# A list scheduler's costs, tolerances and due times in a four-layer transformer kernel

## The chip, the cores and the metric

One core of a Trainium2 chip. The metric is device time in microseconds, the median of repeated executions; lower is better.

## The reference

All is float32. `x` is 8 batches of 512 rows of 512. Four steps, each added to `x` through a layernorm:

```
x = x + LN(attn0(LN(x)))   # scores = xn^T xn (512x512), softmax over rows, xn @ weights^T
x = x + LN(ffn0(LN(x)))    # x @ sum of 8 factors / sqrt(8) + bias
x = x + LN(attn1(LN(x)))   # 8 query heads, 2 key/value heads of 64, softmax, Wo, residual inside
x = x + LN(ffn1(LN(x)))    # silu(x Wg^T * gs) * (x Wu^T * us), then Wd^T * ds; 1408 hidden units, weights -1, 0 or 1
```

`LN` is a layernorm without weights. The weights of the last step hold only -1, 0 and 1.

## The kernel before, in words

**Tiling.** A batch is four tiles of 128 rows by 512. Each of the four steps is a stage function that doesn't issue instructions but records operations: `stage_attn0` (L603 transposes, L642 scores, L671 context), `stage_ffn0` (L603, L693), `stage_attn1` (L855 queries, L825 keys, L836 values, L884 scores of two heads, L915 transposes of their softmax, L946 weighted values, L972 output projection) and `stage_ffn1` (L1094 gate and up products of one slice of 128 hidden units, L1162 down product).

**Tilings and types on TensorE.** Most matmuls use the array as 128x128. The scores of the second attention and their transposes (L884, L915) use it as two halves of 64 rows, `64x128`; the weighted values (L946) as two halves of 64 columns, `128x64`. The last step (L1094, L1162) runs in float32r: each activation is split in two float32r parts (L1035 on ScalarE, L1044 on VectorE), [...] because the weights' low bits are zero. The kernel looks at those bits (`look_at_low_bits`), and a second program in plain float32 stands behind a branch for weights where they aren't; with these inputs it isn't run.

**Vector work.** A layernorm is statistics (L510, L515, or L730, L738), `ve` and a power on GpSimd (L519, L526), normalizing (L534), and the addition to `x` on GpSimd (L553). A softmax is a maximum (L567), the exponential on ScalarE (L574), a reciprocal (L584) and a scaling (L591). ScalarE copies what TensorE transposes from PSUM to SBUF (L607, L927), and computes the sigmoid (L1114); changing between the sigmoid and the exponential loads a table. VectorE gates (L1124, L1133).

**Loads.** SP's queue loads `x`, factors and attention weights and stores the output. GpSimd's queue loads the slices of the gate and up weights (`wgu`, four buffers of 256 KB, L381) and `wd`. PSUM is five banks `f` and three `g`.

**Order.** `Recorder.add` notes an operation with its engine, its estimated duration, what it depends on, and `state`: for ScalarE the table it needs, for TensorE the tiling. Its priority is a due time from `due()`: the batch's number plus a constant of its kind (`DUE`), a shift for some batches (`SHIFT`) and a slope over the steps inside. One unit is one batch. `Recorder.issue` then plans: it keeps a clock for each engine, finds for each ready operation when it could start, takes of each engine's operations those that could start within `SLACK` of the first, and of these the one that is due first. A change of state delays the start by `CHANGE` (1.3 on ScalarE, 0.1 on TensorE), and on TensorE it also counts `STAY` (0.0066) in the priority. The order that comes out is the order in which each engine executes; buffers are assigned in it too. In the last batch (`EARLY`) the second attention and the last step are split into halves of the rows, so the first `FEW` = 4 slices run with 256 columns.

Of the kernel before, what the change touches and what calls it, by code (L numbers as in the profile page):

```python
# [53 lines left out]
class Recorder:  # L54
# [1 line left out]
    LAT = {"PE": 0.22, "ACT": 0.08, "DVE": 0.08, "POOL": 0.08, "SP": 2.6}  # L56
    OWN = 0.05

    CHANGE = {"ACT": 1.3, "PE": 0.1}

    def __init__(self):
        self.ops = []
# [2 lines left out]
    def add(self, eng, dur, fn, reads=(), writes=(), room=(), after=(), state=None, lat=None):  # L65

        op = Op()
        op.eng, op.dur, op.fn, op.state = eng, dur, fn, state  # L70
        op.lat = self.LAT[eng] if lat is None else lat
        op.prio = self.prio
        op.succ, op.wait, op.ready = [], 0, 0.0
        op.n = len(self.ops)
        before = set(after)
        bufs = set(room)
        for ref in reads:
            b, k = ref if isinstance(ref, tuple) else (ref, None)
            bufs.add(b)
            for part, w in b.writers.items():  # L80
                if k is None or part is None or part == k:
                    before.add(w)
            b.readers.setdefault(k, []).append(op)
        for ref in writes:
            b, k = ref if isinstance(ref, tuple) else (ref, None)
            bufs.add(b)
            for part, w in b.writers.items():
                if k is None or part is None or part == k:
                    before.add(w)
            for part, rs in b.readers.items():  # L90
                if k is None or part is None or part == k:
                    before.update(rs)
            if k is None:
                b.writers, b.readers = {None: op}, {}
            else:
                b.writers[k] = op
                b.readers[k] = []
        before.discard(op)
        op.bufs = sorted(bufs, key=lambda b: b.n)
        for b in op.bufs:  # L100
            b.left += 1
        op.wait = len(before)
        for o in sorted(before, key=lambda o: o.n):
            o.succ.append(op)
        self.ops.append(op)
        return op

    def issue(self, places, slack):

        free = {tag: [(0.0, i, t) for i, t in enumerate(ts_)] for tag, ts_ in places.items()}  # L110
        clock = dict.fromkeys(self.LAT, 0.0)
        state = {}
        ready = {e: [] for e in self.LAT}
        for op in self.ops:
            if not op.wait:
                ready[op.eng].append(op)
        left = len(self.ops)
        order = []

        def start(op):  # L120
            at = max(op.ready, clock[op.eng])
            need = {}
            for b in op.bufs:
                if b.t is None:
                    need[b.tag] = need.get(b.tag, 0) + 1
            for tag, n in need.items():
                f = free[tag]
                if len(f) < n:
                    return None
                at = max(at, f[n - 1][0])  # L130
            if op.state is not None and op.state != state.get(op.eng):
                at += self.CHANGE[op.eng]
            return at

        while left:
            best = None
            for e, ops in ready.items():
                able = [(s, op.prio, op.n, op) for op in ops if (s := start(op)) is not None]
                if not able:
                    continue  # L140
                first = min(able)[0]
                held = state.get(e)
                pick = min(
                    (p + (STAY.get(e, 0.0) if op.state not in (None, held) else 0.0), n, s, op)
                    for s, p, n, op in able
                    if s <= first + slack
                )
                if best is None or (pick[2], pick[1]) < best[:2]:
                    best = (pick[2], pick[1], pick[3])
            if best is None:  # L150
                stuck = sorted(
                    (op.prio, e, [b.tag for b in op.bufs if b.t is None])
                    for e, ops in ready.items()
                    for op in ops
                )
                raise RuntimeError(f"no operation can start, for want of buffers: {stuck[:12]}")
            at, _, op = best
            e = op.eng
            ready[e].remove(op)
            for b in op.bufs:  # L160
                if b.t is None:
                    _, _, b.t = free[b.tag].pop(0)
            if op.state is not None:
                state[e] = op.state
            clock[e] = at + op.dur
            end = at + op.dur + op.lat
            op.fn()
            left -= 1
            for b in op.bufs:
                b.left -= 1  # L170
                b.end = max(b.end, end)
                if not b.left:
                    free[b.tag].append((b.end, len(order), b.t))
                    free[b.tag].sort(key=lambda x: x[:2])
            order.append(at)
            for o in op.succ:
                o.wait -= 1
                o.ready = max(o.ready, at + op.dur + self.OWN if o.eng == e else end)
                if not o.wait:
                    ready[o.eng].append(o)  # L180
        return clock
# [61 lines left out]
def layers(  # L243
# [22 lines left out]
    split = flag is not None  # L266
# [97 lines left out]
    fsum = Fixed("fsum", BIG)  # L364
# [7 lines left out]
    wd = Fixed("wd", [P, NI, D], FAST)  # L372
# [185 lines left out]
    def mm(bank, us, go, reads, room=(), state="128x128"):  # L558
        return add("PE", us, go, reads=reads, writes=[bank], room=room, state=state)
# [489 lines left out]
            )  # L1049

    def stage_ffn1(x, b, after):
        PASS = 0.23 if split else 0.86
        xs = [Buf("hl") for _ in range(1 + split)]
        hds = [Buf(f"hd{c}") for c in range(len(CUTS))]

# [6 lines left out]
        known, products = set(), []  # L1062
        for q, (toks, its) in enumerate(rounds):
# [14 lines left out]
            for c, (lo, hi) in enumerate(CUTS):  # L1078
                for it in range(lo, hi):
# [9 lines left out]
                    def product(bank, w, cut=cut):  # L1089
                        def go():  # L1090
                            n = 0
                            for kt in range(KT):
                                for d in xs:
                                    nc.tensor.matmul(  # L1094
                                        bank.t[:, cut],
                                        w.t[:, kt, :],
                                        d.t[:, kt, cut],
                                        start=(n == 0),
                                        stop=(n == KT * len(xs) - 1),
                                    )  # L1100
                                    n += 1

                        return go


                    us = PASS * KT * len(xs) * len(toks) / NT
                    mm(pg, us, product(pg, wg), [wg, *mine], room=[hds[c]])
                    products.append(mm(pu, us, product(pu, wu), [wu, *mine]))
                    gsc = lambda it=it: gs.t[:, it : it + 1]
                    usc = lambda it=it: us_.t[:, it : it + 1]  # L1110
                    add(
# [27 lines left out]
        for t in range(NT):  # L1139
            po = Buf("g")  # L1140
            for c, (lo, hi) in enumerate(CUTS):
# [17 lines left out]
                def down(ops=ops, po=po, lo=lo, hi=hi):  # L1159
# [14 lines left out]
                    reads=[*{buf_of(o): 0 for o in ops}, wd],  # L1174
                    writes=[po],
                    after=products,
                    state="128x128",
                )
            z = Buf("z")
            add(  # L1180
# [36 lines left out]


DUE = {
    "x": (0.0595,),  # L1220
    "fsum": (0.0844, 0.01),
    "scales": (0.2884,),
    "wd": (1.1173,),
    "low": (1.3155, 0.01),
    "a0.norm": (0.0803,),
    "a0.row": (0.0175, 0.0195),
    "a0.out": (0.2134, 0.0139),
    "f0": (0.3719, 0.0331),
    "a1.norm": (0.6166, 0.0452),
    "a1.kv": (0.691,),  # L1230
    "a1.q": (0.6808, 0.1115),
    "a1.row": (0.6967, 0.0723, 0.036, 0.0208),
    "a1.mix": (0.7469, 0.0737, 0.036),
    "a1.out": (1.0283, 0.0236),
    "e1.row": (0.6591, 0.039, 0.1695, 0.0034),
    "e1.mix": (0.9942, 0.0607, 0.1848),
    "e1.out": (0.9884, 0.018, 0.141),
    "f1.norm": (1.7342, 0.0089),
    "f1.gate": (1.716, 0.0146),
    "f1.down": (1.935, 0.019, 0.0131),  # L1240
    "h1.norm": (1.7316, -0.021, 0.095),
    "h1.gate": (1.1851, -0.0129, 0.0932),
    "h1.down": (1.935, 0.0236, 0.0091),
}

SHIFT = {
    ("a0", 0): -0.112,
    ("a1", 0): 0.183,
    ("f0", 0): 0.0174,
    ("f1", 0): -0.0585,  # L1250
    ("a0", 1): -0.1017,
    ("a1", 1): -0.011,
    ("f1", 1): -0.0293,
    ("x", 1): 0.0585,
    ("f1", 2): -0.0302,
    ("f0", -2): 0.0561,
    ("f1", -2): -0.0165,
    ("f0", -1): 0.1176,
}

STAY = {"PE": 0.0066}
SLACK = 0.1198
FSUM_POOL = (0, 3)
EARLY = (-1,)
FEW = 4
# [54 lines left out]
```

## Time and profile before

| | |
|---|---|
| median of 3 runs | 1549.88 us (1546.22 to 1550.55) |
| profiled execution | 1548.17 us |
| its span, first to last instruction | 1546.4 us |
| granted TensorE clock, mean | 0.993 |
| first matmul starts | 7.8 us |
| TensorE busy | 1499.7 us, 8050 matmul records |
| VectorE, ScalarE, GpSimd busy | 1078.3, 688.6, 576.2 us |
| table loads on ScalarE | 60 of 1283 ns |
| DMA moved | 107.98 MB |

The page gives busy time by engine, the same in 40 slices of the span, the chain of work that ended last, and groups of instructions by source line. A float32 matmul leaves two records, a float32r matmul and a transpose one each. The end of a matmul record is modelled, so the distance from one start to the next tells more than a record's length. Line numbers are those of the kernel before; in the kernel after, all the lines named here stand 6 higher (L603 is L609 there).

### The profile page before, as it was taken

The numbers are of one execution on the slowest core, as the hardware profiler recorded it, in microseconds if no ns is written. First come the engines' busy times: TensorE is split into PE (matmuls) and PEld (weight loads), VectorE is DVE, ScalarE is ACT, GpSimd is POOL, SyncE is SP. The second block draws the span as 40 slices with busy tenths as digits, with TensorE's granted clock in tenths as the row PEclk, the third lists the DMA queues.
The fourth block names the chain that finished last, engine by engine and source line by source line (L and its number), as shares of the span: only waits on it lengthen the run. The fifth ranks groups of instructions, "written<-read, shape, count | busy, mean of one in ns | idle before, by whom it ended". The sixth has DMA issues, their size and how long they took to land.

```text
span 1546.4 us, 22104 instructions
## 1 busy us (share of the span) xinstructions
PE 1499.7 (97%) x8050; PEld 927.7 (60%) x8050; DVE 1078.3 (70%) x2227; ACT 688.6 (45%) x1440; POOL 576.2 (37%) x884
## 2 busy tenths in 40 slices
PE   6899999999999999999999999999999999999986
PEld 3454567655666656665566656666566665666675
DVE  5889966778567785587846787467865678558735
ACT  2145537642376324663256523574226642276211
POOL 6803352137411473025720366102651026411431
PEclk9999999999999999999999999999999999999998
DMA  9560054012421125213141122411233002430370
GB/s 332 151 184 8 1 123 82 28 42 62 89 55 36 49 54 104 40 42 75 30 93 35 49 68 55 87 30 49 55 76 75 29 21 58 86 69 21 78 141 30
DMA packets 156695, 107.98 MB, mean 70 GB/s; under 512 B 7073, under 2 KB 137121, under 8 KB 156577
## 3 DMA queue, kind: packets, MB, share of 16 engines
q0 software_dynamic: 98736, 51.13, 17.5%
q1 hardware_dynamic: 57840, 55.34, 11.7%
q8 instruction: 66, 1.08, 0.3%
q14 instruction: 53, 0.43, 0.1%
HBM read 98.06 MB, written 8.39 MB: 69 GB/s over the span
## 4 chain that ended last, share of the span: by engine, by line
PE 74%; POOL 11%; DVE 10%; issue 2%; DMA 2%; ACT 0%; SPq 0%; POOLq 0%; DVEq 0%
PE g L1094 16%; PE g L1162 11%; PE f L884 8%; PE f L946 8%; PE f L855 7%; PE f L972 5%; PE f L915 5%; POOL rstd L526 3%; PE f L642 3%; POOL x L553 3%; PE f L671 3%; DVE row L534 2%; PE f L603 2%; DVE st L510 2%; PE f L836 2%
## 5 line engine op out<-in xcount | busy, mean ns | idle before, releaser
L1094 PE MATMUL g<-hl,wgu 128*128 128x512 f32 (+1 forms) x1408 | 343.2, 395 | 5.5 <-DMA wgu<-in_gate_t 3.3
L1094 PEld LDWEIGHTS g<-hl,wgu 128*128 128x128 f32 x1408 | 254.7, 189 | 80.8 <-issue 12.5
L567 DVE TENSOR_REDUCE s<-f 128x1 f32<-128x512 f32 x288 | 184.8, 684 | 165.3 <-PE f L884 143.4
L519 POOL TENSOR_SCALAR ve<-mv 128x1 f32<-128x1 f32 x224 | 69.5, 311 | 563.7 <-DVE mv L515 534.2
L574 ACT ACTIVATE e<-f,s 128x512 f32<-128x512 f32 x288 | 195.9, 688 | 74.6 <-DVE s L567 73.8
L1162 PE MATMUL g<-wd,hl 128*128 128x512 f32 x704 | 180.6, 407 | 2.2 <-ACT hl L1035 1.7
L553 POOL TENSOR_TENSOR x<-x,z 128x512 f32<-128x512 f32 x120 | 158.1, 1318 | 59.5 <-DVE z L534 38.1
L927 ACT COPY big<-f 128x512 f32<-128x512 f32 x256 | 134.8, 594 | 61.5 <-PE f L915 59.5
L591 DVE TENSOR_SCALAR e<-e,s 128x512 f32<-128x512 f32 x288 | 152.3, 529 | 10.2
L1162 PEld LDWEIGHTS g<-wd,hl 128*128 128x128 f32 x704 | 129.3, 190 | 48.0 <-issue 16.0
L526 POOL TENSOR_TENSOR rstd<-ve,mhalf 128x1 f32<-128x1 f32 x224 | 143.5, 641 | 18.1
L381 POOL DMA_DIRECT2D wgu<-in_gate_t x92 | 73.4, 798 | 167.1 <-PE g L1094 161.8
L884 PE MATMUL f<-kv,big 64*128 64x512 f32 x512 | 132.9, 619 | 0.0
L1124 DVE SCALAR_TENSOR_TENSOR sig<-g,gs,sig 128x512 f32<-128x512 f32 x84 | 62.8, 748 | 95.1 <-ACT sig L1114 95.1
L946 PE MATMUL f<-big,kv 128*64 128x256 f32 x1024 | 124.0, 385 | 0.0
L381 POOL DMA_DIRECT2D wgu<-in_up_t x92 | 70.6, 768 | 129.6 <-PE g L1094 127.7
L693 PE MATMUL f<-fsum,rT 128*128 128x512 f32 x256 | 116.7, 603 | 1.3 <-ACT rT L607 1.2
L855 PE MATMUL f<-big,ws 128*128 128x512 f32 x256 | 118.0, 605 | 0.0
L972 PE MATMUL f<-ws,big 128*128 128x512 f32 x256 | 115.8, 596 | 0.0
L671 PE MATMUL f<-big,big 128*128 128x512 f32 x256 | 114.0, 602 | 0.7 <-ACT big L607 0.7
L946 PEld LDWEIGHTS f<-big,kv 128*64 128x64 f32 x1024 | 68.1, 136 | 68.3 <-issue 19.6
L915 PEld LDWEIGHTS f<-ident,e 64*128 64x128 f32 x2048 | 71.9, 139 | 48.5 <-issue 38.3
(89 smaller groups left out, 1973.8 us busy)
## 6 DMA issues: line engine op xcount, KB each, us to landing
wgu<-in_gate_t POOLq DMA_DIRECT2D x92, 256.0 KB, 3.4
wgu<-in_up_t POOLq DMA_DIRECT2D x92, 256.0 KB, 3.5
x<-in_x SPq DMA_DIRECT2D x32, 256.0 KB, 2.7
ws<-in_wq_t SPq DMA_DIRECT2D x32, 256.0 KB, 2.8
ws<-in_wo_t SPq DMA_DIRECT2D x32, 256.0 KB, 2.6
out<-x SPq DMA_DIRECT2D x32, 256.0 KB, 2.0
hd<-in_factors SPq DMA_DIRECT2D x28, 256.0 KB, 7.2
wd<-in_down_t POOLq DMA_DIRECT2D x11, 256.0 KB, 7.7
```

The lines of the kernel that those rows point to most:

```text
L526: lambda: nc.gpsimd.tensor_tensor(rstd.t[:, :], ve.t[:, :], mhalf, ALU.pow),
L553: lambda: on.tensor_tensor(ap(xt), ap(xt), y.t[:, :], ALU.add),
L567: lambda: nc.vector.tensor_reduce(nmax.t[:, :], sc.t[:, :], AX.X, ALU.max, negate=True),
L574: lambda: nc.scalar.activation(e.t[:, :], sc.t[:, :], AF.Exp, bias=nmax.t[:, :], accum_out=tot.t[:, :]),
L591: lambda: nc.vector.tensor_scalar(e.t[:, :], e.t[:, :], rtot.t[:, :], None, ALU.mult),
L671: nc.tensor.matmul(po.t[:, :], xnT.t[:, j, ts(t, P)], wT.t[:, j, :], start=(j == 0), stop=(j == KT - 1),)
L855: nc.tensor.matmul(pq.t[:, :], wq.t[:, kt, :], hT.t[:, kt, :], start=(kt == 0), stop=(kt == KT - 1),)
L884: nc.tensor.matmul(scs[g].t[:, :], qT.t[gp, i, ts(s, P)], kT.t[gp, :], start=True, stop=True,)
L946: nc.tensor.matmul(po.t[gp, : 2 * P], v.t[:, t * P + g * DH : t * P + (g + 1) * DH], columns_of(aT)[:, g * NT + t, :], start=(t == 0), sto ...
L972: nc.tensor.matmul(po.t[:, :], qT.t[:, i, ts(t, P)], flat(wos[i].t), start=(i == 0), stop=(i == NPAIR - 1),)
L1094: nc.tensor.matmul(bank.t[:, cut], w.t[:, kt, :], d.t[:, kt, cut], start=(n == 0), stop=(n == KT * len(xs) - 1),)
L1162: nc.tensor.matmul(po.t[:, :], ap(o)[:, it - lo, :], wd.t[:, it, :], start=(it == 0 and k == 0), stop=(it == NI - 1 and k == len(ops) - 1),)
```

## The change

Four parts of the scheduler and all its constants.

- `CHANGE` becomes a function of the state before and the new one. On TensorE it counts 0.09 for a change of tiling and 0.12 for an entry to float32r, so up to 0.21; leaving float32r for float32 of the same tiling counts nothing. The products of the last step get the state `128x128r` in the program that runs. Their estimated duration for one pass goes from 0.23 to 0.229.
- In the choice, `STAY` (now 0.2148 on TensorE) is multiplied by this cost, where before 0.0066 was added for any change.
- The tolerance `SLACK` is a number for each engine.
- Operations under 0.3 us have `SMALL` taken off their due time; `SMALL` is 0 in the changed kernel.
- All of `DUE` and `SHIFT` are new numbers.

```diff
-    CHANGE = {"ACT": 1.3, "PE": 0.1}
+    @staticmethod
+    def change(eng, old, new):
+        if new is None or new == old:
+            return 0.0
+        if eng == "ACT":
+            return 1.3
+        return 0.09 * (old is None or old.strip("r") != new.strip("r")) + 0.12 * new.endswith("r")
...
-        op.prio = self.prio
+        op.prio = self.prio - (SMALL if dur < 0.3 else 0.0)
...
-            if op.state is not None and op.state != state.get(op.eng):
-                at += self.CHANGE[op.eng]
-            return at
+            return at + self.change(op.eng, state.get(op.eng), op.state)
...
-                held = state.get(e)
+                stay = STAY.get(e, 0.0)
                 pick = min(
-                    (p + (STAY.get(e, 0.0) if op.state not in (None, held) else 0.0), n, s, op)
+                    (p + stay * self.change(e, state.get(e), op.state), n, s, op)
                     for s, p, n, op in able
-                    if s <= first + slack
+                    if s <= first + slack[e]
                 )
...
-        PASS = 0.23 if split else 0.86
+        PASS, array = (0.229, "128x128r") if split else (0.86, "128x128")
...
-                    mm(pg, us, product(pg, wg), [wg, *mine], room=[hds[c]])
-                    products.append(mm(pu, us, product(pu, wu), [wu, *mine]))
+                    mm(pg, us, product(pg, wg), [wg, *mine], room=[hds[c]], state=array)
+                    products.append(mm(pu, us, product(pu, wu), [wu, *mine], state=array))
...
 DUE = {
-    "x": (0.0595,),
-    "fsum": (0.0844, 0.01),
+    "x": (-0.2533,),
+    "fsum": (0.3114, 0.0312),
...
-    "e1.row": (0.6591, 0.039, 0.1695, 0.0034),
+    "e1.row": (0.0386, 0.0334, 0.5419, -0.0515),
...
-    "h1.gate": (1.1851, -0.0129, 0.0932),
+    "h1.gate": (1.4039, 0.0198, 0.4807),
...
-STAY = {"PE": 0.0066}
-SLACK = 0.1198
+STAY = {"PE": 0.2148}
+SLACK = {"PE": 0.1422, "ACT": 0.1218, "DVE": 0.1385, "POOL": 0.1719, "SP": 0.1357}
+SMALL = 0
```

The down product's `state="128x128"` also becomes `state=array`. `SHIFT` goes from 12 entries to 19.

More of the change, by code (lines that the diff above doesn't have):

```diff
@@ L1176, in stage_ffn1 @@
                     after=products,
-                    state="128x128",
+                    state=array,
                 )
@@ L1219 @@
 DUE = {
-    "x": (0.0595,),
-    "fsum": (0.0844, 0.01),
[L1222 to L1234, printed above, removed]
-    "e1.row": (0.6591, 0.039, 0.1695, 0.0034),
@@ L1236 @@
[L1236 to L1241, printed above, removed]
-    "h1.gate": (1.1851, -0.0129, 0.0932),
-    "h1.down": (1.935, 0.0236, 0.0091),
+    "x": (-0.2533,),
+    "fsum": (0.3114, 0.0312),
+    "scales": (0.6222,),
+    "wd": (1.213,),
+    "low": (1.2859, 0.014),
+    "a0.norm": (0.0439,),
+    "a0.row": (0.0055, 0.0111),
@@ new lines @@
+    "a0.out": (0.1758, 0.0279),
+    "f0": (0.2466, 0.1151),
+    "a1.norm": (0.6218, 0.0433),
+    "a1.kv": (0.7585,),
+    "a1.q": (0.695, 0.101),
+    "a1.row": (0.7101, 0.0703, 0.0322, 0.0233),
+    "a1.mix": (0.6497, 0.0532, 0.0436),
+    "a1.out": (1.0313, 0.0174),
+    "e1.row": (0.0386, 0.0334, 0.5419, -0.0515),
+    "e1.mix": (1.0181, 0.019, 0.1484),
+    "e1.out": (0.6386, 0.0105, 0.1575),
+    "f1.norm": (1.9819, 0.0044),
+    "f1.gate": (1.7154, 0.0078),
+    "f1.down": (1.9213, 0.0376, 0.0083),
@@ L1244 @@
+    "h1.norm": (1.0667, -0.2027, 0.1913),
+    "h1.gate": (1.4039, 0.0198, 0.4807),
+    "h1.down": (1.9405, 0.0086, 0.0044),
 }
 SHIFT = {
[L1247 to L1258, printed above, removed]
-}
-STAY = {"PE": 0.0066}
-SLACK = 0.1198
+    ("a0", 0): 0.072,
@@ new lines @@
+    ("a1", 0): 0.2005,
+    ("f0", 0): 0.0598,
+    ("f1", 0): -0.0823,
+    ("x", 0): 0.0884,
+    ("a0", 1): -0.0745,
+    ("f0", 1): -0.1916,
+    ("f1", 1): 0.0114,
+    ("x", 1): 0.1766,
+    ("a0", 2): 0.0102,
+    ("f0", 2): -0.1129,
+    ("x", 2): -0.2536,
+    ("a1", -2): 0.0132,
+    ("f1", -2): -0.0341,
+    ("x", -2): 0.0641,
+    ("a1", -1): -0.0323,
+    ("f0", -1): 0.112,
+    ("f1", -1): -0.1277,
+    ("x", -1): 0.134,
+}
+STAY = {"PE": 0.2148}
+SLACK = {"PE": 0.1422, "ACT": 0.1218, "DVE": 0.1385, "POOL": 0.1719, "SP": 0.1357}
```

## The prediction

> **What bounds the kernel now.** I read the page's first two parts, the waits of TensorE, TensorE's timeline in one batch, then the chain. The lines of the page:
>
> ```profile
> PE 1499.7 (97%) x8050; PEld 927.7 (60%) x8050; DVE 1078.3 (70%) x2227; ACT 688.6 (45%) x1440; POOL 576.2 (37%) x884
> ...
> PE   6899999999999999999999999999999999999986
> DVE  5889966778567785587846787467865678558735
> ```
>
> TensorE (PE) is at nine tenths in all slices but the first two and last two. Next comes what it still waits for:
>
> ```profile
> PE f L603 <- DVE row L534: 12.8, 12, 3.4
> PE f L603 <- DVE big L534: 7.8, 1, 7.8
> PE f L603 <- DVE e L591: 3.6, 3, 1.7
> PE g L1094 <- DMA wgu<-in_gate_t: 3.3, 4, 1.3
> ```
>
> 7.8 us are the start; the rest is mostly the first batch (gaps of 3.4, 1.7 and 2.2 us up to 208 us) and the tail (1.0, 1.3, 0.7, 0.6, 1.3 us from 1465 us). In the steady batches I find one gap of 0.67 us each (L1094 to L603). The windows say the same: 198.8 of 200 us busy. So no wait is worth much in the steady part; only a shorter TensorE program is. "Busy" hides pauses between matmuls, so I took starts. TensorE's timeline, columns start, length, line, tiling, shape, records:
>
> ```profile
> 406.88 0.60 PE L603 MATMUL f<-ident,row 128*128 128x128 f32 x4
> 407.24 2.10 PE L1094 MATMUL g<-hl,wgu 128*128 128x512 f32 x8
> 409.17 3.60 PE L855 MATMUL f<-big,ws 128*128 128x512 f32 x8
> 412.61 3.60 PE L825 MATMUL f<-big,ws 128*128 128x512 f32 x8
> ...
> 427.28 1.21 PE L915 MATMUL f<-ident,e 64*128 64x64 f32 x32
> 428.42 2.12 PE L1094 MATMUL g<-hl,wgu 128*128 128x512 f32 x8
> 430.47 1.99 PE L884 MATMUL f<-kv,big 64*128 64x512 f32 x8
> ```
>
> ```profile
> 475.50 0.71 PE L915 MATMUL f<-ident,e 64*128 64x64 f32 x16
> 476.14 3.70 PE L855 MATMUL f<-big,ws 128*128 128x512 f32 x8
> 479.77 0.71 PE L915 MATMUL f<-ident,e 64*128 64x64 f32 x16
> 480.32 1.96 PE L884 MATMUL f<-kv,big 64*128 64x512 f32 x8
> ```
>
> The same group L855 takes 412.61 - 409.17 = 3.44 us start to start between groups of its own tiling (128*128), and 479.77 - 476.14 = 3.63 us between two of 64*128. It is entered and left by a change, and each change splits over its two groups: 0.09 us where one is left (L915: 0.64 us before L855, 0.55 us before L884 of its own tiling), the rest, about 0.10, at the first matmul after it. So **one change of tiling costs about 0.20 us** when it enters a 128*128 group. The float32r product L1094 agrees: 430.47 - 428.42 = 2.05 us for 8 passes between changes. Entered from a float32 group of the same tiling it takes 1.93 us, but the L603 ahead of it is shorter (0.36 us where four of 0.109 us make 0.44), so 1.85 net, against 8 x 0.229 = 1.83: **the entry to float32r by itself costs about 0.02 us**, not the 0.12 that the new model counts.
>
> [...]
>
> **The change part by part.** No arithmetic, tile or buffer changes; only the order on each engine. So I built the changed program and counted in its order.
>
> 1. *Changes of tiling* in the program that runs (the fallback behind the check of low bits doesn't): 345 before, 303 after. Into 128*128 (both data types) 137 to 117, into 64*128 147 to 125, into 128*64 61 to 61. A steady batch has 45 before and 39 after. The 20 into 128*128 at 0.20 us make -4.0. The 22 into 64*128 lie between 0.10 (only the leaving is seen for L915) and 0.20: -2.2 to -4.4, and I take the middle, -3.3. TensorE is the bound, so all of it is on the path: **-7.3 us**, ends -6.2 and -8.4.
> 2. *Entries to float32r*: 140 to 103, but those from float32 of the same tiling, the only ones not counted above, 43 to 40: 3 x 0.02, nothing. If the 0.12 of the model were right, -0.4.
> 3. *Short operations first*: SMALL is 0, so no priority moves. This part does nothing: 0.
> 4. *Table loads of ScalarE*: 60 to 50, -12.8 us of ScalarE, which is 45% busy. Off the path: 0. Its cover is TensorE's continuous work; were it gone, 1.3 us each.
> 5. *Tolerances and due times* move everything else, so waits come and go. Steady batch: the transposes of the second of the last three attention rows stood 11.6 us of matmuls after the product they depend on and waited 0.67 us; they get 13.9 us, so that wait goes (seen in 4 batches, -2.7). The transposes of the fourth row ahead of the factor product (L693) had 11.6 us after the end of their L671 group and get 7.7. Their chain, read in the timeline at 1107.5 to 1116.4 (statistics, POOL's power, normalizing, POOL's add, the same again), takes 8.9 us, but the new order puts two vector operations that stood ahead of it behind it: estimate +0.4 us in 6 or 7 batches, +2.6, ends 0 and +8. Together about 0.
> 6. *Queues*. SP's first 19 loads keep their order; the second batch's x moves ahead of three small constants, all well before use. POOL's weight loads (0.8 us to issue, 3.4 to land) follow the products. The new order has longer unbroken runs of L1094: 152 passes in the first batch where the longest before was 48, 40 to 72 later, 192 in the tail where 176 stood. One buffer's cycle is 1.83 us of use, 0.3 to the issue, 3.44 to landing, 0.14 to the start: 5.7 us, and four buffers give 4 x 1.83 = 7.3. So 1.6 us of slack for a late issue: 0, at worst +1 per turn of four in the long run of 19 slices, +5.
> 7. *Tail*. 16 half-width passes (1.9 us) move from between the last two projections to behind the last row's transposes, where TensorE waited for the copies: -1.9. But ten half-width slices now follow each other, 4 x 0.96 = 3.8 us for a cycle of 4.8: about +1 twice. Net 0, ends -2 and +3.
>
> Sum: -7.3 + 0 + 0 + 0. I add +0.3 for a few waits I can't place: -7. The profiled run took 1548.17 us (span 1546.4 and 1.8 around it), 1.7 below the median of the runs shown: **1541 us**.
>
> **The rivals.**
> *The gain is eaten by waits.* Parts 5 to 7 at their upper ends are +8, +5, +3; half of these is +8, so about 1548. For it: the new order sometimes has less cover, and rows waiting for L534 are already the largest wait. Against: where I measured cover, it shrank in one place and grew in another.
> *ScalarE is late at one place, and the kernel slower.* In 20 places (three in each steady batch) the new order has attention transposes L915, two score matmuls L884, and at once the next L915 into a bank that the first L915 filled. In the trace the first of the two copies L927 ends 0.84 us after the last transposes start, the second 1.33; the L884 pair covers about 1.0. The bank reused is that of the first copy, so nothing waits if ScalarE is idle then. If an exponential (0.69 + 0.20 us) stands ahead, each place waits 0.84 + 0.89 - 1.0 = 0.73 us, 20 x 0.73 = 14.6: 1548.2 - 7.3 + 14.6 = 1555.5. It decides from 0.37 us a place. Against: in the order of ScalarE the exponential or copy ahead of it has 2 us of matmuls to finish in.
> *More is gained than the changes.* The start and the first batch hold some 15 us of gaps; a better overlap there (the first L1094 comes after 17 us more of other matmuls, so the rows ahead of it are less urgent) gives -6 more: 1535.
> *The change does not do what it says*: of its named parts one is idle (part 3) and one misprices (0.12 for 0.02); the count of changes nevertheless falls, so this doesn't end at no change by itself.
>
> **How the numbers follow.** Against the median of 1549.88, 0.3% is 4.6 us, about what a measurement here can tell from no change. Forecast, 1537 to 1545: 0.56. More gained, under 1537: 0.12. Eaten, 1545 to 1554: 0.20. Slower, over 1554.5: 0.12. So faster 0.68, same 0.20, slower 0.12. The range leaves out the best twentieth or so and the slower case: 1533 to 1551.
>
> **What would show it.** Right: a steady batch, from its first L825 to the next one's (969.99 to 1156.73 us in the chain, so 186.7), at about 185.5 us with the same number of passes, 50 table loads, L855 still 3.44 and 3.63 us. L603's waits for L534 stay near 13 us. Wrong: new lines among TensorE's waits, such as L915 for ACT's L927, L1094 for the DMA above 5 us, or L603 for L534 above 18 us. If the time falls by much more than 8 us, the price of a change or the gaps of the first batch were undercounted.

## The result, and the profile after

| | before | after |
|---|---|---|
| median | 1549.88 us | 1530.61 us (1527.48 to 1531.42, 5 runs) |
| ratio after to before | | 0.9881, 95% interval 0.9865 to 0.9896 |
| profiled execution, its span | 1548.17, 1546.4 us | 1531.37, 1529.6 us |

The kernel is 1.2% faster, 19.3 us by the medians and 16.8 us by the two profiled executions. The forecast was 8.9 us less by the medians and 7 by the profile. The direction is right, the size is less than half of it, and 1530.6 lies below the range. The sums below are made on the two profiled executions.

The page after, the lines that answer to those shown of before (all lines of code stand 6 higher):

```profile
PE 1485.2 (97%) x8050; PEld 926.3 (61%) x8050; DVE 1078.3 (70%) x2227; ACT 677.2 (44%) x1430; POOL 577.8 (38%) x884
...
PE   6899999999999999999999999999999999999987
...
DVE  5889964788547785588845978459874678657745
```

The same 8050 records keep TensorE busy 14.5 us less, at the same 97%. So most of the gain doesn't show as idle time on this view: it is inside "busy". The waits of TensorE after:

```profile
PE f L609 <- DVE big L540: 10.6, 2, 9.3
PE f L609 <- DVE row L540: 6.1, 10, 1.5
PE f L609 <- DVE e L597: 5.6, 10, 1.7
PE g L1100 <- DMA wgu<-in_gate_t: 2.3, 2, 1.5
```

Rows waiting for the layernorm fell from 12.8 us to 6.1, the longest from 3.4 to 1.5; the start (9.3 of the first line) came 1.4 later. That is no effect of the change: tail_out and tail_fill below, whose order in the head is the after's matmul for matmul, start at 9.1 and 8.4 us, and fill_before, with the order of before, at 9.1 where before has 7.8. TensorE's timeline in a steady batch, with start, length, line, tiling, shape and records:

```profile
421.98 1.21 PE L921 MATMUL f<-ident,e 64*128 64x64 f32 x32
423.12 3.70 PE L861 MATMUL f<-big,ws 128*128 128x512 f32 x8
426.75 1.95 PE L952 MATMUL f<-big,kv 128*64 128x256 f32 x16
428.62 1.56 PE L890 MATMUL f<-kv,big 64*128 64x512 f32 x6
```

L861 between two changes takes 426.75 - 423.12 = 3.63 us, as L855 did before: the price of a change is what it was, there are fewer of them.

Then the granted clock, which the prediction read only as a mean (0.993; after 0.995). Laid over the timeline it has stretches of 3.4 us at 0.5, that is at half clock. Between the first and the last matmul there are 17.1 us of them before (three stretches, up to 88 us, and 1473.5 to 1476.9 and 1514.5 to 1517.9 in the tail) and 6.8 us after (30.2 to 37.1). As an estimate, from the 22.39 and 20.83 us of the last L1162 group with and without a stretch (before and fill_before, below), a stretch takes about half of its length from the matmuls. The first four lines are the two stretches in the tail of before and the 3.5 us ahead of each, where TensorE (the first busy time of a line) is busy for only 1.69 and 1.29 us; the last two are stretches with waits in the tail of after. The column behind POOL is the granted clock:

```profile
1473.50:1476.90 3.40, 3.06 (x15) 3.05 (x15) 0.78 (x2) 0.47 (x1) 0.81 (x1) 0.50 0.00 0
1514.50:1517.90 3.40, 3.40 (x9) 2.64 (x8) 0.00 (x0) 0.00 (x0) 0.00 (x0) 0.50 0.00 0
1470.00:1473.50 3.50, 1.69 (x9) 1.02 (x9) 2.05 (x4) 1.17 (x2) 1.05 (x3) 1.00 0.88 153
1511.00:1514.50 3.50, 1.29 (x5) 0.53 (x4) 2.61 (x4) 1.00 (x2) 0.00 (x0) 0.99 0.00 0
```

```profile
1457.00:1461.00 4.00, 2.79 (x24) 2.55 (x23) 2.95 (x6) 1.65 (x3) 2.25 (x4) 1.00 1.02 193
1498.00:1502.00 4.00, 3.06 (x13) 2.51 (x14) 1.64 (x3) 1.14 (x2) 0.00 (x0) 1.00 0.00 0
```

**Where the 16.8 us went**, by kind. "Idle" is the sum of the gaps between matmul records:

| | before | after | us |
|---|---|---|---|
| first matmul starts | 7.84 us | 9.29 us | +1.4 |
| changes of tiling | 345 | 303 | -7.5 |
| idle of TensorE behind the first matmul | 29.1 us | 25.3 us | -3.8 |
| time at half clock, half of it lost | 17.1 us | 6.8 us | -5.1 |
| not placed | | | -1.8 |

The -7.5 is the sum of the prices of all boundaries as their starts show them (0.094 us where a tiling is left, 0.05 to 0.11 at the first matmul of the next). At a flat 0.20 a change it would be -8.4, and 0.9 unplaced. Of the -5.1, the tail makes 3.4. The 1.7 of the head (10.2 us at half clock before, 6.8 after) are within chance, like the start: with the after's order in the head, tail_out has 10.2 us there and tail_fill 3.4, and fill_before, with the order of before, has 6.8.

And by place, cut at the first L825 (L831) of each batch (the content makes up what is missing to 16.8); "content" is what the matmuls in a stretch take at the pace they have inside long groups, since the order moves some from batch to batch:

| stretch | before | after | of it content | net |
|---|---|---|---|---|
| start to batch 1 | 89.27 us | 91.11 us | +0.4 | +1.4 |
| batch 1 to 2 | 112.55 | 112.96 | +0.4 | 0 |
| batch 2 to 3 | 210.79 | 203.24 | -4.1 | -3.4 |
| batches 3 to 8, five | 930.85 | 927.47 | +4.9 | -8.3 |
| tail, behind batch 8 | 193.10 | 185.03 | -1.9 | -6.2 |

### The profile page after: what moved, and what is told of

It reads as the page before. It is cut to its first block, busy times and chain, and to the rows that moved or that the text cites. A ratio compares the mean times of both kernels' runs of the same rounds, so it can differ in the third digit from the quotient of the medians.

```text
span 1529.6 us, 22123 instructions
## 1 busy us (share of the span) xinstructions
PE 1485.2 (97%) x8050; PEld 926.3 (61%) x8050; DVE 1078.3 (70%) x2227; ACT 677.2 (44%) x1430; POOL 577.8 (38%) x884
## 4 chain that ended last, share of the span: by engine, by line
PE 82%; DVE 8%; POOL 6%; DMA 2%; issue 2%; ACT 0%; SPq 0%; POOLq 0%; DVEq 0%; ACTq 0%
PE g L1100 21%; PE g L1168 11%; PE f L890 8%; PE f L952 8%; PE f L861 7%; PE f L699 6%; PE f L921 5%; PE f L978 4%; PE f L609 3%; PE f L648 3%; POOL rstd L532 3%; PE f L842 2%; PE f L677 2%; PE f L831 2%; DVE st L516 2%; DVE row L540 2%
## 5 line engine op out<-in xcount | busy, mean ns | idle before, releaser
L1100 PE MATMUL g<-hl,wgu 128*128 128x512 f32 (+1 forms) x1408 | 332.8, 391 | 2.6 <-DMA wgu<-in_gate_t 2.3
L1100 PEld LDWEIGHTS g<-hl,wgu 128*128 128x128 f32 x1408 | 255.9, 188 | 73.4 <-DVE s L573 10.6
L559 POOL TENSOR_TENSOR x<-x,z 128x512 f32<-128x512 f32 x120 | 163.4, 1361 | 93.3 <-DVE z L540 78.0
L597 DVE TENSOR_SCALAR e<-e,s 128x512 f32<-128x512 f32 x288 | 171.8, 597 | 10.2
L1168 PE MATMUL g<-wd,hl 128*128 128x512 f32 x704 | 176.0, 402 | 1.4 <-DVE hl L1050 1.4
L861 PE MATMUL f<-big,ws 128*128 128x512 f32 x256 | 116.7, 599 | 0.5 <-ACT e L580 0.5
L677 PE MATMUL f<-big,big 128*128 128x512 f32 x256 | 114.9, 606 | 1.3 <-ACT big L613 0.7
L921 PEld LDWEIGHTS f<-ident,e 64*128 64x128 f32 x2048 | 74.7, 139 | 46.8 <-issue 27.0
```

What stands on the lines that cost most here:

```text
L559: lambda: on.tensor_tensor(ap(xt), ap(xt), y.t[:, :], ALU.add),
L597: lambda: nc.vector.tensor_scalar(e.t[:, :], e.t[:, :], rtot.t[:, :], None, ALU.mult),
L861: nc.tensor.matmul(pq.t[:, :], wq.t[:, kt, :], hT.t[:, kt, :], start=(kt == 0), stop=(kt == KT - 1),)
L1100: nc.tensor.matmul(bank.t[:, cut], w.t[:, kt, :], d.t[:, kt, cut], start=(n == 0), stop=(n == KT * len(xs) - 1),)
L1168: nc.tensor.matmul(po.t[:, :], ap(o)[:, it - lo, :], wd.t[:, it, :], start=(it == 0 and k == 0), stop=(it == NI - 1 and k == len(ops) - 1),)
```

## The experiments

The theories at the start: (A) the changes of tiling give about 7 us, and the due times the rest, by waits of the tail and of batch 2 that go, with the half clock that stood behind them; (B) the new cost function makes the gain, since it gives orders that wait less; (C) a change costs about 0.4 us, so that 42 explain it alone.

**What a change of tiling costs.** One more small matmul ahead of each factor product and each context product, in another tiling or in the same:

```diff
+                nc.tensor.matmul(
+                    po.t[:, :64], xnT.t[:64, 0, :], fsum.t[:64, 0, :64], start=True, stop=True
+                )
```

The same stands ahead of the context product, with `wT` in place of `fsum`. Tile_same has `[:128, 0, ...]` in both operands.

> The kernel after, with one more float32 matmul of 64 columns at the head of each L699 product and each L677 product, on 64 rows, that is in another tiling than its neighbours (its result is overwritten; the outputs stay). 64 such matmuls, of which 58 stand between matmuls of 128*128 and so add two changes of tiling each, 116 in all. To be read against the run with the same matmul on 128 rows. If a change costs 0.15 to 0.20 us of TensorE, as the prediction took it, this run is 17 to 23 us longer than that one; by the planner's own 0.09 it is 10 us longer; if a change hides behind other work, 0 to 5 us.

> The same 64 extra matmuls on 128 rows, in the tiling of their neighbours: no further change. They are short (2 records of 64 columns each, about 0.11 us by the transposes' 0.109 us a record), so 6 to 13 us over the kernel after, 1537 to 1544 us, if nothing else moves.

Measured: 1555.55 us (1553.98 to 1557.07) and 1539.32 us (1537.65 to 1541.10), which is 1.0049 (1.0032 to 1.0067) and 0.9944 (0.9925 to 0.9962) of before. The difference of 16.2 us over 116 changes is 0.14 us. Tile_other happened to have 1.8 us less idle time and 3.4 us less at half clock (lost: 1.7), so its matmuls took 18.5 us more from the first to the last (15.0 + 1.8 + 1.7): **0.16 us a change**. TensorE's timeline of tile_other shows one (L701 is the extra matmul, L705 the factor product): the product takes 563.86 - 560.23 = 3.63 us, where the after's L861 ahead of a group of its own tiling takes 3.43.

```profile
559.87 0.43 PE L701 MATMUL f<-fsum,rT 64*128 64x64 f32 x2
560.23 3.70 PE L705 MATMUL f<-fsum,rT 128*128 128x512 f32 x8
563.86 0.43 PE L701 MATMUL f<-fsum,rT 64*128 64x64 f32 x2
```

Theory C is out: 42 changes at 0.20 make 8.4 us, not 16.8. So is the planner's 0.09 for a change, which would have been 10 us here.

**One part of the change alone.** Due_only is the kernel after with the cost model of before:

```diff
-        return 0.09 * (old is None or old.strip("r") != new.strip("r")) + 0.12 * new.endswith("r")
+        return 0.1
...
-        PASS, array = (0.229, "128x128r") if split else (0.86, "128x128")
+        PASS, array = (0.23, "128x128") if split else (0.86, "128x128")
...
-STAY = {"PE": 0.2148}
+STAY = {"PE": 0.066}
```

Cost_only is the kernel after with `DUE`, `SHIFT` and the one tolerance of before. True_price is the kernel after with the prices that I had measured, in the cost function alone:

```diff
-        return 0.09 * (old is None or old.strip("r") != new.strip("r")) + 0.12 * new.endswith("r")
+        return 0.2 * (old is None or old.strip("r") != new.strip("r")) + 0.02 * new.endswith("r")
```

> The kernel after with the old cost of a change (0.1 for any change of tiling, nothing for an entry to float32r, a penalty of 0.0066 in the choice), but the new due times, shifts and tolerances. It has 308 changes of tiling where the kernel after has 303 and the one before 345. Theory A (42 fewer changes are worth about 7 us, and the new due times take the rest out of the tail, the waits of the second and third batch, and the pauses after which TensorE runs at half clock): within 3 us of the kernel after, 1529 to 1534 us. Theory B (the new cost function makes the gain, by orders that wait less): back by half or more of the 19 us, 1540 us or above. Theory C (a change of tiling costs twice what I took, 0.4 us): 1533 us.

> The kernel after with the due times, shifts and the single tolerance 0.1198 of the kernel before; the new cost function and its weight 0.2148 stay. It has 305 changes of tiling. Theory A: the changes' 7 us are gained, the rest isn't, and due times that were chosen for another order may add waits: 1539 to 1550 us. Theory B (the cost function makes the gain): 1530 to 1535 us. Theory C (0.4 us for a change): 1533 us, since 40 of the 42 changes are gone.

> The kernel after with the prices that I read from the trace of before in the cost function: 0.2 for a change of tiling, 0.02 for an entry to float32r. All else as after. The order then has 254 changes of tiling. Theory A: 49 fewer changes give 7 to 10 us, if no waits are added: 1521 to 1524 us; each new wait takes from that. Theory C (0.4 us): 1511 us. Rival: the due times fit the prices they were chosen with, and the new order waits more than it saves: above 1531 us.

Measured: due_only 1600.97 us (ratio 1.0339, 1.0319 to 1.0360), cost_only 1554.42 us (1.0043, 1.0026 to 1.0060), true_price 1664.66 us (1.0752, 1.0732 to 1.0772). Each alone is slower than before, though all three have fewer changes than it (308, 305 and 254), and true_price has the fewest and is the slowest of all. What they have is waits, in due_only and true_price most of all of the row transposes for the layernorm; the first line of TensorE's waits in due_only and in true_price, to be read against 12.8 us before and 6.1 after:

```profile
PE f L609 <- DVE row L540: 20.9, 18, 3.4
```

```profile
PE f L609 <- DVE row L540: 74.2, 25, 10.3
```

In cost_only one of them takes 5.57 us in batch 2, and the pace behind it shows the half clock: four transposes take 1.12 us where they take 0.60 to 0.66 at the full clock (the granted clock from 385 to 410 us is 0.80 in the mean). TensorE's timeline there:

```profile
388.28 1.53 PE L609 MATMUL f<-ident,row 128*128 128x128 f32 x12 [0.63 <-DVE row L540]
395.38 1.12 PE L609 MATMUL f<-ident,row 128*128 128x128 f32 x4 [5.57 <-DVE row L540]
397.01 1.97 PE L609 MATMUL f<-ident,row 128*128 128x128 f32 x8 [0.51 <-DVE row L540]
```

By place the two halves of the change part clearly. "Excess" is the time of a stretch over its content, in us:

| stretch | before | after | cost_only | due_only |
|---|---|---|---|---|
| batch 2 to 3 | 14.1 | 10.6 | 25.6 | 22.0 |
| batches 3 to 8, five | 56.4 | 48.0 | 49.2 | 107.3 |
| tail | 22.0 | 15.8 | 22.7 | 14.9 |

The gain of the steady batches comes with the cost function (7.2 of the 8.4 us are there without the new due times and tolerances), the gain of the tail with the due times and tolerances (all of it is there without the new cost function). But each half, without the other, loses more elsewhere than it gains: batch 2 in cost_only, the five batches in due_only. So A and B each hold for a place, and neither for the whole. What made true_price slow isn't isolated: the price stands in the planned start and, times `STAY`, in the choice, where the weight of a change goes from 0.019 to 0.043 of a batch and that of an entry to float32r from 0.026 to 0.004.

**Small constants.** Each is the kernel after with one setting changed:

```diff
-SLACK = {"PE": 0.1422, "ACT": 0.1218, "DVE": 0.1385, "POOL": 0.1719, "SP": 0.1357}
+SLACK = {"PE": 0.1198, "ACT": 0.1198, "DVE": 0.1198, "POOL": 0.1198, "SP": 0.1198}
```

> The kernel after with the one tolerance of before (0.1198) for all engines; cost function and due times stay. 312 changes where the kernel after has 303. If the due times and the cost function carry the gain and the tolerances are a small matter, 1531 to 1534. If the order is brittle, so that the constants hold together only as a set, row transposes wait for the layernorm in new places: over 1540, with half clock behind the waits. The prediction's part 5 (tolerances and due times move waits with no net effect) gives about 1532.

```diff
-SMALL = 0
+SMALL = 0.05
```

> The kernel after with SMALL at 0.05 of a batch in place of 0, so that operations under 0.3 us really go first; 308 changes of tiling against 303. By the count of changes alone, 1531 to 1532. If short vector operations taken first shorten the layernorm chains, fewer waits for them, 1526 to 1530. If the constants only fit together as a set, row transposes wait in new places, with half clock behind them: 1540 to 1610.

```diff
-    "fsum": (0.3114, 0.0312),
+    "fsum": (0.0844, 0.01),
```

> The kernel after with one constant of before: the due time of the factors' loads and sums, (0.0844, 0.01) in place of (0.3114, 0.0312). This work is done once, in the first batch. 310 changes against 303. If a due time acts where its work stands, the wait of 1.40 us for the factors at 53 us goes and the rest stays: 1529 to 1531.5. If any constant moves the whole order, later batches differ too, and their waits: over 1540.

Measured: slack_one 1602.63 us (1.0357, 1.0335 to 1.0379), small05 1554.66 us (1.0040, 1.0026 to 1.0054), fsum_old 1548.58 us (1.0008, 0.9996 to 1.0020). The count of changes (9, 5 and 7 more, at most 1.8 us) doesn't explain 72, 24 and 18 us; idle time and half clock do, as the account below shows. The prediction's way of treating tolerances and due times, a sum of a few waits near zero, isn't fit for constants that move the whole order.

Fsum_old has two lessons, and neither expectation held as a whole. The loss stands where the work stands: from batch 2 on its stretches are the after's (203.20, 188.57, 184.79, 184.85, 191.99, 177.50 us), so one constant doesn't move everything. But the place is worse, not better. The waits of TensorE, and VectorE's timeline at the start:

```profile
PE f L609 <- DVE big L540: 21.1, 2, 13.0
```

```profile
9.21 0.18 DVE L521 BATCH_NORM_AGGREGATE mv<-st 128x2 f32<-128x6 f32 x1
18.61 3.97 DVE L419 TENSOR_TENSOR fsum<-fsum,hd 128x512 f32<-128x512 f32 x4 [9.22 <-DMA hd<-in_factors]
22.50 0.54 DVE L540 TENSOR_SCALAR big<-x,mv,rstd 128x512 f32<-128x512 f32 x1
```

The sums of the factors (L419) now stand on VectorE ahead of the normalizing that the transposes need, and wait 9.2 us for their loads; L540 waits behind them, and TensorE for L540, 13.0 us. Here a due time that was too early for its data delayed what was queued behind it.

**The tail and the half clock.** Tail_out is the kernel after with the six due times `e1.*` and `h1.*` of before, the ones that only the last batch has:

```diff
-    "e1.row": (0.0386, 0.0334, 0.5419, -0.0515),
+    "e1.row": (0.6591, 0.039, 0.1695, 0.0034),
...
-    "h1.gate": (1.4039, 0.0198, 0.4807),
+    "h1.gate": (1.1851, -0.0129, 0.0932),
```

> The kernel after with the due times of the last batch's split steps (the kinds that begin with e1 and h1) of the kernel before. It has 306 changes of tiling. Theory A (6 us of the gain lie in the tail, from the last output projection to the end, where waits are shorter and TensorE's clock isn't halved): the tail gets longer by 2 to 6 us and the rest stays, 1533 to 1537 us. Theory C (all lies in the changes): 1530 to 1532 us.

Measured: 1539.26 us (1536.99 to 1541.73), ratio 0.9942 (0.9919 to 0.9965). Up to the tail the order is the after's, matmul for matmul, and the batches from the first on take what they take there, to 0.1 us; the tail takes 194.14 us where the after's takes 185.03. So these six constants are worth **9.1 us**. There are 10.2 us at half clock in this tail and none in the after's, which makes 5.1; of the other 4.0, 3.7 are idle time (9.5 us in this tail, 5.8 in the after's).

Then I filled the waits of this tail, and of the tail of before, with idle matmuls, whose result is overwritten by what follows, to see whether the half clock follows the waits:

```diff
+            for n in range(fill):
+                nc.tensor.matmul(
+                    pt.t[:, :], wd.t[:, n, :P], wd.t[:, n, :], start=True, stop=True
+                )
             for c in range(KT):
                 nc.tensor.transpose(blocks(pt.t)[:, c, :], ap(src)[:, ts(c, P)], ident)
```

In tail_fill 8 and then 2 of them stand ahead of the transposes of the last two rows, in the order in which these run, 2 ahead of the first late product and 8 ahead of the first down product; in fill_before 6, 2, 4 and 8.

> The kernel with the tail's due times of before (1539.26 us, two stretches of half clock in the tail of 6.8 and 3.4 us), with 20 idle float32r matmuls of 0.23 us in four places of the tail where TensorE waits, overwritten by what follows. If the half clock follows the waits and costs half of its stretch, the stretches go and the time falls by about 5 us to 1534, the row transposes still ending when the layernorm lets them. If the clock falls for another reason, or the waits alone make the tail's 9 us, it stays at 1538 to 1541, or rises by the matmuls that don't fit into the waits (up to 4.6 us).

> The kernel before, with 20 idle float32r matmuls of 0.23 us (4.6 us) put into four places of the tail where TensorE waits (1.3, 0.7, 0.7 and 1.7 us; the rest of them stands in front of waits of 0.5 us or more); what follows overwrites their results. Nothing else moves. The kernel before has two stretches of half clock there, 1473.5 to 1476.9 and 1514.5 to 1517.9 us. If these follow from the waits and cost half of their length, at most 3.4 us come back, less what of the idle matmuls doesn't fit into the waits: 1544.5 to 1547 against 1548.5, and the last L1162 group takes 20.9 us where it took 22.4. If the half clock isn't caused by the waits, the stretches stay, and the time is 1548 to 1551.

Measured: tail_fill 1536.73 us (1536.42 to 1537.46; ratio 0.9925, 0.9908 to 0.9942), fill_before 1545.33 us (ratio 0.9983, 0.9974 to 0.9991). In fill_before both stretches of the tail are gone, **2.6 us faster with 20 matmuls more**. TensorE's timeline at the end of before, and of fill_before (L1162 is L1176 there), then two windows of fill_before where the stretches were, at full clock; behind 57 us it has no half clock at all:

```profile
1513.18 0.49 PE L1162 MATMUL g<-wd,hl 128*128 128x512 f32 x1 [1.71 <-ACT hl L1035]
1514.17 22.39 PE L1162 MATMUL g<-wd,hl 128*128 128x512 f32 x87 [0.50 <-DVE hl L1044]
```

```profile
1509.80 1.99 PE L1171 MATMUL g<-wd 128*128 128x512 f32 x8
1511.68 0.50 PE L1176 MATMUL g<-wd,hl 128*128 128x512 f32 x1
1512.67 20.83 PE L1176 MATMUL g<-wd,hl 128*128 128x512 f32 x87 [0.50 <-DVE hl L1048]
```

```profile
1473.50:1476.90 3.40, 2.72 (x18) 2.47 (x19) 1.27 (x3) 0.77 (x2) 0.81 (x1) 1.00 0.00 0
1511.50:1514.90 3.40, 2.90 (x13) 2.01 (x12) 0.96 (x1) 0.13 (x1) 0.00 (x0) 1.00 0.02 5
```

Eight idle matmuls in place of the 1.71 us, and the 87 records behind them take 20.83 us instead of 22.39. The tail takes 189.37 us where it took 193.10, and all batches from the first on what they took, to 0.1 us. In tail_fill the second stretch went the same way, the first only shrank from 6.8 to 3.4 us: the wait for the row that comes last got no shorter than 1.39 us, since only 2 matmuls stood there and 8 ahead of the row that needed less. The median is 2.5 us lower, half of what I expected, but the two ratios to before overlap, and the profiled tail fell by 1.2 us only (194.14 to 192.94), so this gain isn't clear of noise. That the pauses bring the half clock is shown: of the five stretches of 3.4 us in the two tails four went when the pauses were filled, and nothing else was changed; and the mean clock over all executions rose from 0.9915 (26 of before) to 0.9943 (13 of fill_before), and from 0.9930 to 0.9955 (4 each) with tail_fill. One stretch costs about 1.6 us (22.39 - 20.83), near half of its 3.4.

**The head.** The same in the first batch of the kernel after, where its only half clock is:

```diff
-            transpose_to(column(wT, i), whole(e))
+            transpose_to(column(wT, i), whole(e), fill=xn if b == 0 and i in (0, 2) else None)
```

> The kernel after, with one idle float32 matmul of 0.86 us in each of two waits of the first batch (1.63 us at 22.3, 1.69 us at 27.2), overwritten by what follows. If these waits bring the half clock of 30.2 to 37.1 us, it goes, and the L677 group behind it takes 13.8 us in place of 16.6. Whether the kernel gains by it: 2.8 us (1527 to 1528) if nothing is late behind it; nothing (1529.5 to 1531.5) if the sums of the factors, which TensorE waits for at 53.4 us, come when they came. I expect nothing. If the half clock stays, the clock doesn't follow the waits.

Measured: 1529.31 us (1528.32 to 1529.80), ratio 0.9887 (0.9871 to 0.9904) where the kernel after has 0.9881: no difference that can be told. One stretch is left where after had two (30.9 to 34.3 us), but tail_fill, with nothing filled in the head, also has only one there, so this isn't shown to be the fill's doing. The context products (L677; L681 there) take 15.70 us instead of 16.57. Their timeline lines, and the wait for the factors behind them:

```profile
30.42 15.70 PE L681 MATMUL f<-big,big 128*128 128x512 f32 x32 [0.67 <-ACT big L617]
...
52.50 1.12 PE L703 MATMUL f<-fsum,rT 128*128 128x512 f32 x2 [1.40 <-POOL fsum L419]
```

My reason for "nothing" was wrong: the factors did not keep their time, the wait for them is still 1.40 us and moved up with the rest. From the first matmul to the last this run took 1508.4 us, the after's 1510.5; but such a difference between two executions isn't more than runs differ. Whether the head's half clock costs anything, and whether these two waits bring it, stays open. No version here is shown to beat the kernel after.

**All runs in one account.** From the first matmul to the last, against the kernel after (1510.5 us): the difference in idle time, half of the difference in time at half clock, and 0.20 us a change, against what was measured.

| | idle | half clock | changes | sum | measured |
|---|---|---|---|---|---|
| before | +3.8 us | +5.1 us | +8.4 us | +17.3 us | +18.2 us |
| tail_out | +1.0 | +6.8 | +0.6 | +8.4 | +8.3 |
| fsum_old | +13.5 | 0 | +1.4 | +14.9 | +16.3 |
| small05 | +13.7 | +8.5 | +1.0 | +23.2 | +22.6 |
| cost_only | +11.7 | +8.5 | +0.4 | +20.6 | +23.3 |
| slack_one | +37.6 | +18.8 | +1.8 | +58.2 | +69.0 |
| due_only | +39.4 | +22.2 | +1.0 | +62.6 | +71.2 |
| true_price | +92.5 | +49.5 | -9.8 | +132.2 | +135.3 |

Three terms carry between 84 and 103% of every difference. In the three slowest the half clock adds about half of what the waits last. In fsum_old it adds nothing to 13.5 us of waits, in tail_out 6.8 to 1.0: it matters where the waits stand. Up to 2.7 us of a row's idle time and 1.7 of its half clock can be chance: by so much the head differs between tail_out and after, which have one order there.

## Why the prediction was wrong

By its own parts:

1. *Changes of tiling*, -7.3: right. The starts give -7.5, and the inserted changes 0.14 to 0.16 us each, inside its 0.10 to 0.20. The middle value for the 22 into 64*128 was a guess that came out: 0.094 us at the leaving side and 0.05 at the entry.
2. *Entries to float32r*, 0: nothing in the traces speaks against it, but no run tried the entry alone.
3. *Short operations first*, 0: right for `SMALL` = 0. Set to 0.05 it costs 24 us.
4. *Table loads*, 0: 50 as counted; TensorE's waits name ScalarE no more than before.
5. *Tolerances and due times*, "Together about 0": **failed** by about 2.7 us. In the five steady batches it set a wait that goes against one that comes (-2.7 and +2.6). The first went as forecast (four waits of 0.66 to 0.68 us). The other came smaller: the rows waited 1.9 us in all after. All idle time went from 5.2 to 3.5 us, and with 31 changes fewer (-6.2 at 0.20) this makes 7.9 of the 8.3. And it summed steady batches only: the wait of 2.24 us at 205 us, which it had read and counted to the first batch, is gone (idle in batch 2 to 3: 3.1 to 0.9 us), and 1.3 us of new waits came in batch 1 to 2 (0.3 to 1.6).
6. *Queues*, 0: right. No wait for the weights is over 1.55 us. Those inside the long run of the tail come to 1.5 us and belong to part 7.
7. *Tail*, "Net 0, ends -2 and +3": **failed, the largest miss**: -6.2. The waits of TensorE in the tail, before and then after:

```profile
PE g L1094 <- DMA wgu<-in_gate_t: 2.9, 3, 1.3
PE f L603 <- DVE row L534: 2.0, 2, 1.3
PE g L1162 <- ACT hl L1035: 1.7, 1, 1.7
PE g L1094 <- ACT hl L1035: 0.7, 1, 0.7
PE g L1162 <- DVE hl L1044: 0.5, 1, 0.5
PE g L1094 <- DVE hl L1044: 0.3, 1, 0.3
```

```profile
PE g L1100 <- DMA wgu<-in_gate_t: 2.3, 2, 1.5
PE g L1168 <- DVE hl L1050: 1.4, 1, 1.4
PE f L609 <- DVE row L540: 1.2, 1, 1.2
PE f L1100 <- DMA wgu<-in_up_t: 0.7, 2, 0.4
```

   The copies cost 3.2 us before and 1.4 after, near the -1.9, but in part by luck: behind the last row's transposes, the place it named, 1.0 us went (0.67 and 0.34); the other 0.8 went ahead of the down product (1.71 and 0.50 before, 1.36 after), waits that its list of gaps leaves out. The loads cost 2.9 and 3.0: in the run of ten slices 1.5 us came, near the feared +2, but two waits of before (0.60 and 1.26) went, which it hadn't counted. The rows gave another -0.8. And the two stretches of half clock behind the waits of before went, 3.4 us, a term that isn't in the prediction at all: it took a wait to cost its length.

So the step that failed is the sum of the waits (parts 5 and 7, set at 0), in size and in what a wait costs. Changes -7.3 and waits about 0 should have been changes -7.5 to -8.4, waits -3.8 and half clock -3.4 in the tail. The start (+1.4) and the half clock of the head (-1.7) are within chance and nearly cancel; 0.9 to 1.8 us stay without a cause. The medians differ by 2.5 us more than the two profiled executions; the median of 48 further executions of before is 1547.8 us, against which the gain is 17.2.

The rivals: waits eating the gain, and ScalarE late at L915, did not come (no wait of L921 for ScalarE is among the listed ones). (In the sum of the first, 1548.2 - 7.3 + 8 is 1549, not 1548.) "More is gained" had the right sign and mostly the wrong place: of the gaps that it counted to the start and the first batch only the 2.2 us at 205 us went. That the change doesn't do what it says is true in part: its prices (0.09, 0.12) are not those seen in the runs (0.14 to 0.20; for the entry the prediction's estimate of 0.02), and with 0.2 and 0.02 in their place the planner makes a kernel 134 us slower. In every run that put back or altered a part of the set, the kernel became slower.

What it named as signs: the steady batch came to 185.5 us, as named, but as the mean of five with 1.0 us more matmuls in each, so that 184.5 is the like; L603's waits were to stay near 13 us and fell to 6.1. "If the time falls by much more than 8 us, the price of a change or the gaps of the first batch were undercounted": in the main neither was it.

## What to carry to other kernels

Where TensorE is the bound, lay the granted clock over the timeline before summing; a mean of 0.993 hid, at half of 17.1 us, some 8.5 us. Ask how much idle time a change leaves within 3.4 us: in the tail of before 2.2 us of short waits that lay that close together cost about 1.6 us more than their length; in the tail of after, with at most 1.55 us in any 3.4 us, the clock stayed at 1.00. When a planner's constants change, count what the new order leaves behind each vector chain at every place, the tail and the early batches as carefully as the steady ones, because a change of tiling fewer is worth 0.14 to 0.20 us and one transpose that stood too early waited 5.6. A part of such a set, tried alone, tells where a gain stands but not what it is worth.

## What the runs showed of the hardware

- *Half clock after short pauses.* Ahead of the stretches in the tail of before the longest pause was 1.71 us, and the pauses came in pieces, with matmuls between. The traces of before and after show what amount was enough there. In before the granted clock goes from 1.00 to 0.50 at 29.7, 50.1, 84.3, 1473.5 and 1514.5 us, for 3.41 us each; these times are 5, 11, 21, 428 and 440 times 3.413 us from 12.6 us, where its record begins at 1.00. In after it goes to 0.50 at 30.2 us, 5 times 3.413 us from 13.2 us, for 6.83. Cut into pieces of 3.413 us from there, the two executions have 5 pieces at full clock with TensorE idle for 1.9 us or more (2.1 to 2.8), and the next piece ran at half clock after all 5; of 859 with under 0.95 us, after none; of the 16 between, after one (it had 1.72 us; after one with 1.74 us the clock stayed). In before, 2.2 us of its waits fell into the piece ahead of 1514.5 us; the 1.55 and 1.21 us of waits in the tail of after, between 1453 and 1458.5 us, fell into different pieces, with 1.1 and 1.2 us of idle time, and it kept its clock. Wherever the cuts are laid over these two tails, a piece of before holds at most 2.2 us of idle time, one of after 1.55.
- *The stretches lie differently in each execution.* The first of these cuts behind the first matmul comes 1.3 us after it in before, and in after, tail_out and tail_fill, with one order in the head, 0.5, 1.4 and 3.1 us after it; their heads had 6.8, 10.2 and 3.4 us at half clock. So one order has more half clock in one execution than in another. The time follows: in 48 executions of before the mean clock ran from 0.988 to 0.994; the 11 at 0.994 took 1546.2 us on average, the 5 at 0.988 or 0.989 took 1551.1.
- *A change of tiling.* In before, from the start of a group's last matmul to the start of the next group it takes 0.094 us more where that has another tiling, and the first matmul there takes 0.05 to 0.11 us more. The changes inserted in tile_other cost 0.14 us each by the medians, 0.16 with idle time and half clock levelled.
- *A pause can be filled.* In fill_before, 20 matmuls whose result nobody reads, in the waits, kept the clock (1.00 where both stretches of the tail were) and made the kernel faster by 0.17% (0.09 to 0.26).
